# Scores of a spiking recommender on one core: the last time step by pieces, loads by three parts with 24 successive rows per partition

## The chip, the cores and the metric

The kernel runs on one core of a Trainium2 chip. The metric is the device time of one execution in microseconds (us). Before the change it is 1647.41 us, the median of three runs from 1646.87 to 1650.15.

## What is computed

A batch of B = 1024 users has T = 50 item numbers each; a table has N = 100001 items with D = 128 values. The reference, cut to what matters:

```python
emb = emb_table.at[0].set(0.0)
prefix = jnp.cumsum(emb[seq], axis=1)
denom = jnp.minimum(arange(1, T + 1)[None, :], lengths[:, None])
uF = prefix / denom[:, :, None]
y = (uF - uF.mean(axis=0)) * rsqrt(uF.var(axis=0) + 1e-5) * gamma + beta   # over the batch
def step(v, x):                     # 50 steps, one after the other
    v = v + (x - v) / 2.0
    spike = (v >= 1.0)
    return v - spike, spike
scores = spikes.mean(axis=0) @ emb.T          # [1024, 128] @ [128, 100001]
```

The output is 1024 x 100001 float32 values, 409.6 MB.

## The kernel before, in words

**First stage, 50 steps.** D lies on the 128 partitions and the 1024 users on the free axis. For each step `gather` issues eight indirect DMAs from POOL (L198), one for each 128 users. PE transposes each gathered block of 128 x 128 into the running sums `pre[0]` and `pre[1]` (L307), two PSUM tiles of 512 columns. For each half DVE scales the sums to `uF` (L316) and takes batch statistics (L317); it joins them to mean and variance `mv` (L327). ACT takes the square root (L331) and subtracts the mean from all 1024 columns (L332). DVE takes the reciprocal, improves it by one Newton step and makes the scale `a` (L340 to L346, on 128 x 1 columns), ACT applies the scale (`x`, L350), and DVE adds the old potential (`step`, L353), which it holds as `negv = s - v` (L359; L302 in the last step). `s` are the spikes of the step before (L337; L301 in the last step), which `counted` adds up in PSUM by a matmul (L275).

In the last step `s` and `negv` are made whole at the head (L301, L302). At its end the work after `a` goes by three groups of 128, 512 and 384 columns. `countA`, `countB` and `countC` are the final spike counts (`spiked`, L286) that the second stage needs as weights. `warm` (L376) is 16 transposes whose output nobody reads, in the PSUM tile v0.

**Second stage, 98 parts.** The table is cut into parts of 1024 rows (`HALF`); the last has 673. A part in SBUF is turned by PE (L128) and split by ACT and DVE into a high and a low half (`prepare`, L150 and L151), and each of the eight groups of 128 users is multiplied by both (`product`, L158). A product of 128 users by 1024 rows lies in one of four PSUM tiles, and DVE and ACT in turn scale it and write it to `o` in SBUF (L467 and L469). When all parts of a chunk are written for a group of users, one store on SP's queue brings `o` to memory (L167). `WIDTHS` gives the parts of each chunk: 4 chunks of 2, 4 of 3, 11 of 6 and 3 of 4. From the ninth chunk on, three buffers `o` of six parts take turns.

**Loads.** `fetch` loads table rows (L106). The first 38 parts (`HELD`) are loaded on SP's queue in the first stage, the other 60 by loads of three parts on ACT's queue, in the user groups n = 1 and n = 4 of the chunks. Partition p gets rows 8p to 8p + 7 of each part, which is 4096 bytes in a row in memory. So a transposed part has its columns in the order of k and p, and the split reads PSUM in an order that puts them right (`views`). The end of the last part is loaded by single rows of 512 bytes (L115, L120).

**Order.** The program fixes the order on each engine by hand. DMAs from SP and ACT use eight DMA semaphores in turn: an issue waits until the DMA that had its semaphore before it has landed.

The functions that the change touches:

Of the kernel before, what the change touches and what calls it, by code (L numbers as in the profile page):

```python
# [12 lines left out]
F32 = mybir.dt.float32  # L13
# [5 lines left out]
ALU = mybir.AluOpType  # L19

P = 128
BN_EPS = 1e-5
V_TH = 1.0
HALF = 1024
KQ = HALF // P
BANK = 512
GROUP = 6
AHEAD = 6
LATE = 2
HELD = AHEAD * GROUP + LATE  # L30

WIDTHS = 4 * [2] + 4 * [3] + 11 * [6] + [4, 4, 4]
NARROW, MIDDLE = 4, 8


# [1 line left out]
def rec_kernel(  # L37
# [9 lines left out]
    nc = tc.nc  # L47
    B, T = seq.shape
    N, D = table.shape
    NB = B // P  # L50
# [13 lines left out]
    countA = const.tile([P, P], F32R, tag="countA", name="countA")  # L64
# [9 lines left out]
    parts = -(-N // HALF)  # L74
    assert sum(WIDTHS) == parts
    rows = {}
    split = {}

    free = [
        [embp.tile([P, HALF], F32R, tag=f"{x}{i}", name=f"{x}_{i}") for x in ("hi", "lo")] for i in range(2)  # L80
    ]

    def size(q):
        return min(HALF, N - q * HALF)
# [14 lines left out]
    def fetch(r, q, n):  # L99

        engine = nc.sync if q < HELD else nc.scalar
        k = slot(q)[1]
        n = min(n, parts - q)
        whole = n - (size(q + n - 1) < HALF)
        if whole:
            engine.dma_start(  # L106
                out=r[:, k : k + whole, :],
                in_=table[q * HALF : (q + whole) * HALF, :].rearrange("(q p k) d -> p q (k d)", p=P, k=KQ),
            )
        if whole < n:  # L110
            full, rest = divmod(size(parts - 1), P)
            c1 = (parts - 1) * HALF
            r = r[:, k + whole, :].rearrange("p (k d) -> p k d", d=D)
            if full:
                engine.dma_start(  # L115
                    out=r[:, :full, :],
                    in_=table[c1 : c1 + full * P, :].rearrange("(k p) d -> p k d", p=P),
                )
            if rest:
                engine.dma_start(out=r[:rest, full, :], in_=table[c1 + full * P : N, :])  # L120
# [49 lines left out]
    with ExitStack() as ph:  # L170
# [23 lines left out]

        def gather(t):
            es[t] = gp.tile([P, B], F32, tag="e", name=f"e_{t}")
            for n in range(NB):
                nc.gpsimd.indirect_dma_start(  # L198
                    out=es[t][:, n * P : (n + 1) * P],
                    out_offset=None,  # L200
                    in_=table,
                    in_offset=bass.IndirectOffsetOnAxis(ap=idx[:, n, t : t + 1].bitcast(U32), axis=0),
                )
# [81 lines left out]
        def spiked(out, cs, v):  # L285
            nc.vector.scalar_tensor_tensor(out, v, V_TH, count[:, cs], ALU.is_ge, ALU.add)  # L286

        whole = slice(0, B)
        halves = [slice(h * BANK, (h + 1) * BANK) for h in range(B // BANK)]
        v = None  # L290
# [3 lines left out]
        for t in range(T):  # L294
            last = t == T - 1
            if t + 1 < T:
                gather(t + 1)
            e = es.pop(t)
            if last:
                s = lp.tile([P, B], BF16, tag="s", name=f"s_{t - 1}")  # L300
                nc.vector.tensor_single_scalar(s, v, V_TH, ALU.is_ge)  # L301
                nc.vector.tensor_tensor(negv, s, v, ALU.subtract)  # L302
            uF = up.tile([P, B], F32, tag="uF", name=f"uF_{t}")
            bs = sp.tile([P, B // BANK, 6], F32, tag="bs", name=f"bs_{t}")
            for h, cs in enumerate(halves):
                for k in range(0, BANK, P):
                    nc.tensor.matmul(  # L307
                        pre[h][:, k : k + P],
                        lhsT=e[:, h * BANK + k : h * BANK + k + P],
                        rhs=ident,  # L310
                        start=False,
                        stop=last,
                        is_transpose=True,
                        skip_group_check=True,
                    )
                nc.vector.scalar_tensor_tensor(uF[:, cs], rlen[:, cs], 1.0 / (t + 1), pre[h], ALU.max, ALU.mult)  # L316
                nc.vector.bn_stats(bs[:, h, :], uF[:, cs])  # L317
            if not last:
                correct(t + 1, l)
            else:  # L320

                counted(t - 1, s)
                count = once.tile([P, B], F32, tag="zT", name="count")
                for h, cs in enumerate(halves):
                    nc.scalar.copy(count[:, cs], sums[h])
            mv = sp.tile([P, 2], F32, tag="mv", name=f"mv_{t}")
            nc.vector.bn_aggr(mv, bs.rearrange("p h s -> p (h s)"))  # L327


            r = sp.tile([P, 1], F32, tag="r", name=f"r_{t}")  # L330
            nc.scalar.activation(r, mv[:, 1:2], AF.Sqrt, bias=eps)  # L331
            nc.scalar.activation(uF, uF, AF.Identity, bias=mv[:, 0:1], scale=-1.0)  # L332


            if t and not last:
                s = lp.tile([P, B], BF16, tag="s", name=f"s_{t - 1}")
                nc.vector.tensor_single_scalar(s, v, V_TH, ALU.is_ge)  # L337
                counted(t - 1, s)

            nc.vector.reciprocal(r, r)  # L340
            q = sp.tile([P, 1], F32, tag="q", name=f"q_{t}")
            nc.vector.tensor_mul(q, r, r)
            nc.vector.scalar_tensor_tensor(q, mv[:, 1:2], BN_EPS, q, ALU.add, ALU.mult)
            nc.vector.tensor_scalar(q, q, -0.5, 1.5, ALU.mult, ALU.add)
            a = sp.tile([P, 1], F32, tag="a", name=f"a_{t}")
            nc.vector.tensor_scalar(a, q, r, hgb[:, 0:1], ALU.mult, ALU.mult)  # L346


            def x(vt, cs):
                nc.scalar.activation(vt, uF[:, cs], AF.Identity, bias=hgb[:, 1:2], scale=a)  # L350

            def step(vt, cs):
                nc.vector.scalar_tensor_tensor(vt, negv[:, cs], -0.5, vt, ALU.mult, ALU.add)  # L353

            if not last:
                vt = vp.tile([P, B], F32, tag=f"v{t % 2}", name=f"v_{t}")
                x(vt, whole)
                if t:
                    nc.vector.tensor_tensor(negv, s, v, ALU.subtract)  # L359
                step(vt, whole)  # L360
                v = vt
                if t + 2 < T:
                    l = only(t + 2)

                if t in (T - 8, T - 6):
                    q = (t - T + 8) // 2
                    prepare(q, vp.tile([P, HALF], F32, tag="v1", name=f"pt_{q}"))
                    fetch(tiles[0], GROUP + q, 1)
                    rows[GROUP + q] = tiles[0][:, q, :]
# [1 line left out]

        warm = vp.tile([P, HALF], F32, tag="v0", name="warm")
        for k in range(2 * KQ):
            nc.tensor.transpose(warm[:, k % KQ * P : (k % KQ + 1) * P], ident, ident)  # L376
        vC = vp.tile([P, B - BANK - P], F32, tag="v1", name="vC")
        groups = [
            (slice(0, P), pre[0][:, :P], countA),
            (slice(P, P + BANK), pre[1], countB),  # L380
            (slice(P + BANK, B), vC, countC),
        ]
        for cs, vt, _ in groups:
            x(vt, cs)
        cs, vt, first = groups[0]
        step(vt, cs)
        spiked(first, cs, vt)
        for cs, vt, _ in groups[1:]:
            step(vt, cs)
        for cs, vt, c in groups[1:]:  # L390
# [26 lines left out]
    to_fetch = HELD  # L417
# [5 lines left out]
    for c, W in enumerate(WIDTHS):  # L423
# [30 lines left out]
        for n in range(NB):  # L454
# [5 lines left out]
            for q in range(q0, q1):  # L460
                h0 = (q - q0) * HALF
                hw = size(q)
                po = psum.tile([P, HALF], F32, tag="ps", name=f"po_{n}_{q}")
                for k0 in range(0, hw, BANK):
                    product(po[:, k0 : k0 + BANK], q, n, k0, min(BANK, hw - k0))
                if turn % 2 == 0:
                    nc.vector.tensor_scalar_mul(o[:, h0 : h0 + hw], po[:, :hw], 1.0 / T)  # L467
                else:
                    nc.scalar.mul(o[:, h0 : h0 + hw], po[:, :hw], 1.0 / T)  # L469
                turn += 1  # L470
                if c == 0 and n == 1:
                    store(n, q * HALF, o[:, h0 : h0 + hw])
                if n == NB - 1:
                    free.append(split.pop(q))
                    ready()
# [5 lines left out]
            if n in (1, 4) and c >= MIDDLE and to_fetch < parts:  # L481
                g, k = slot(to_fetch)
                if k or to_split >= (g - 1) * GROUP + LATE:
                    if k == 0:
                        r = group(g)
                    fetch(r, to_fetch, GROUP // 2)
                    to_fetch += GROUP // 2
        assert to_split == q2
        q0 = q1

# [18 lines left out]
```

## Time and profile before

The profiled execution took 1574.98 us, of which the span from the first to the last instruction is 1573.2 us. It is 72.4 us below the median of the three runs; the profile doesn't show why.

| what | where | time |
|---|---|---|
| first stage, up to the first store's issue | timeline | 511.6 us |
| POOL busy with gathers (L198) | page, part 5 | 377.8 us, 400 of 945 ns |
| DVE evictions (L467) | page, part 5 | 464.1 us, 391 of 1220 ns |
| ACT evictions (L469) | page, part 5 | 388.1 us, 391 of 1019 ns |
| stores, DMA queue q1 | page, part 3 | 429.81 MB with the first loads |
| late loads, DMA queue q10 | page, part 3 | 31.28 MB |
| memory rate from 718 to 1436 us | windows | 424 GB/s, DMA share 1.00 |

A row of part 5 gives line, engine, operation, output and input with shapes, and count; then busy time and the mean of one; then the idle time before them and who ended it. In part 2 each digit is a slice of 39.3 us.

### The profile page before, as it was taken

Reading aid. Unit: us, or ns where it says so; the run is one execution under the profiler, and the core shown is the slowest. Engines: PE = TensorE matmul, PEld = TensorE weight load, DVE = VectorE, ACT = ScalarE, POOL = GpSimd, SP = SyncE. Lnnn points to the kernel's source line nnn. Section 1 sums busy time; section 2 is a strip of 40 time slices with the busy share of each in tenths; the row PEclk is TensorE's granted clock in tenths of the full one; section 3 lists DMA queues with packets and bytes.
Section 4 is the critical chain, followed back from the end, with each engine's and each line's share of the span. In section 5 each row is a group of like instructions: output and inputs, shape, how many; then the busy total and the mean of one; then the engine's idle time right before and its main releaser. Section 6 shows DMA issues by size and latency. Waiting matters only on the chain.

```text
span 1573.2 us, 12601 instructions
## 1 busy us (share of the span) xinstructions
PE 1147.9 (73%) x4538; PEld 817.6 (52%) x4548; DVE 942.1 (60%) x1161; ACT 630.6 (40%) x700; POOL 378.5 (24%) x406
## 2 busy tenths in 40 slices
PE   4555555555555998889878878887888778777885
PEld 2222222222233776668667666666666667665763
DVE  4777777777777665667555545545555555554553
ACT  2322222222233554555444444444444444443442
POOL 6777777777776000000000000000000000000000
PEclk9999999999999999999999999999999999999998
DMA  9622222222221999999999999999999999999898
GB/s 338 247 53 53 53 53 52 53 53 53 53 79 45 385 416 403 423 417 402 426 429 428 430 427 424 421 415 428 418 428 423 414 428 410 426 424 426 362 423 371
DMA packets 54859, 488.14 MB, mean 310 GB/s; under 512 B 12139, under 2 KB 12940, under 8 KB 32524
## 3 DMA queue, kind: packets, MB, share of 16 engines
q1 hardware_dynamic: 33424, 429.81, 65.1%
q0 software_dynamic: 12800, 26.24, 6.3%
q10 hardware_dynamic: 8572, 31.28, 5.0%
q8 instruction: 36, 0.59, 0.1%
q14 instruction: 27, 0.22, 0.0%
HBM read 77.69 MB, written 409.60 MB: 310 GB/s over the span
## 4 chain that ended last, share of the span: by engine, by line
DMA 50%; POOL 19%; PE 11%; issue 10%; ACT 5%; DVE 4%; another core or an unknown queue 0%; DVEq 0%; ACTq 0%; SPq 0%; POOLq 0%
DMA scores<-o 46%; POOL e L198 19%; PE po L158 10%; ACT o L469 4%; DMA e<-in_L_rec_emb_table,idx 3%; DVE o L467 2%; DMA rows<-in_L_rec_emb_table 2%; PE pt L128 1%; PE pre L307 0%; ACT pairs L150 0%; DVE s L337 0%; DVE bs L317 0%; DVE uF L316 0%; DVE pairs L151 0%; DMA idx<-in_r_seq 0%
## 5 line engine op out<-in xcount | busy, mean ns | idle before, releaser
L467 DVE TENSOR_SCALAR o<-po 128x1024 f32<-128x1024 f32 x391 | 464.1, 1220 | 354.3 <-DMA scores<-o 314.5
L469 ACT ACTIVATE o<-po 128x1024 f32<-128x1024 f32 (+1 forms) x391 | 388.1, 1019 | 548.9 <-DMA scores<-o 336.2
L198 POOL DMA_INDIRECT e<-in_L_rec_emb_table,idx x400 | 377.8, 945 | 124.5 <-issue 116.4
L158 PE MATMUL po<-pairs,countB 128*128 128x512 f32 x1136 | 304.6, 415 | 69.0 <-ACT o L469 52.1
L158 PEld LDWEIGHTS po<-pairs,countB 128*128 128x128 f32 x1136 | 218.5, 197 | 132.0 <-ACT o L469 66.8
L307 PE MATMUL pre<-ident,e 128*128 128x128 f32 x400 | 156.2, 452 | 152.4 <-DMA e<-in_L_rec_emb_table,idx 149.0
L158 PE MATMUL po<-pairs,countC 128*128 128x512 f32 x852 | 230.4, 416 | 49.3 <-ACT o L469 49.3
L158 PEld LDWEIGHTS po<-pairs,countC 128*128 128x128 f32 x852 | 163.6, 198 | 94.2 <-ACT o L469 60.5
L307 PEld LDWEIGHTS pre<-ident,e 128*128 128x128 f32 x400 | 79.2, 200 | 246.1 <-DMA e<-in_L_rec_emb_table,idx 223.6
L151 DVE TENSOR_TENSOR pairs<-pt,pairs 128x1024 fp32r<-128x1024 f32 x71 | 86.3, 1222 | 91.3 <-ACT pairs L150 91.2
L331 ACT ACTIVATE r<-mv,eps 128x1 f32<-128x1 f32 x50 | 14.7, 295 | 305.5 <-DVE mv L327 305.5
L316 DVE SCALAR_TENSOR_TENSOR uF<-rlen,pre 128x512 f32<-128x512 f32 x100 | 68.4, 684 | 108.3 <-PE pre L307 108.2
L128 PE MATMUL pt<-ident,rows 128*128 128x128 f32 x782 | 111.7, 290 | 9.7 <-ACT o L469 5.1
L128 PEld LDWEIGHTS pt<-ident,rows 128*128 128x128 f32 x782 | 100.3, 152 | 29.9 <-issue 8.8
L158 PE MATMUL po<-hi,countB 128*128 128x512 f32 x216 | 89.5, 414 | 15.8 <-ACT o L469 12.6
L264 PE MATMUL pre<-zT,l 128*128 128x512 f32 x100 | 78.1, 783 | 18.9 <-DVE uF L316 18.8
L275 PE MATMUL sums<-s,ident_h 128*128 128x512 bf16 x88 | 45.4, 607 | 60.6 <-DVE s L337 60.6
L158 PE MATMUL po<-lo,countB 128*128 128x512 f32 x216 | 86.5, 402 | 0.0
L158 PE MATMUL po<-pairs,countA 128*128 128x512 f32 x284 | 71.7, 395 | 9.3 <-ACT o L469 9.2
L150 ACT CAST pairs<-pt 128x1024 fp32r<-128x1024 f32 x71 | 71.8, 1012 | 15.0 <-PE pt L128 14.8
L158 PE MATMUL po<-hi,countC 128*128 128x512 f32 (+1 forms) x162 | 67.8, 418 | 11.7 <-ACT o L469 11.7
L350 ACT ACTIVATE v<-uF,hgb,a 128x1024 f32<-128x1024 f32 x49 | 59.2, 1208 | 37.6 <-DVE a L346 37.5
(76 smaller groups left out, 841.9 us busy)
## 6 DMA issues: line engine op xcount, KB each, us to landing
scores<-o SPq DMA_DIRECT2D x88, 3072.0 KB, 20.3
scores<-o SPq DMA_DIRECT2D x32, 1536.0 KB, 8.9
scores<-o SPq DMA_DIRECT2D x16, 2048.0 KB, 12.6
scores<-o SPq DMA_DIRECT2D x30, 1024.0 KB, 8.6
rows<-in_L_rec_emb_table ACTq DMA_DIRECT2D x19, 1536.0 KB, 29.3
rows<-in_L_rec_emb_table SPq DMA_DIRECT2D x6, 3072.0 KB, 25.3
scores<-o SPq DMA_DIRECT2D x8, 1872.5 KB, 11.3
e<-in_L_rec_emb_table,idx POOLq DMA_INDIRECT x400, 2.5
```

Source lines behind the costliest of these rows:

```text
L128: nc.tensor.transpose(pt[:, k0 : k0 + kw], r[:kw, k0 : k0 + D], ident[:kw, :kw])
L150: nc.scalar.copy(vh, vp)
L151: nc.vector.tensor_tensor(vl, vp, vh.bitcast(F32), ALU.subtract)
L158: nc.tensor.matmul(po[:, :kw], lhsT=counts[n], rhs=part[:, k0 : k0 + kw], start=j == 0, stop=j == 1,)
L198: nc.gpsimd.indirect_dma_start(out=es[t][:, n * P : (n + 1) * P], out_offset=None, in_=table, in_offset=bass.IndirectOffsetOnAxis(ap=idx[: ...
L264: nc.tensor.matmul(pre[h], lhsT=l, rhs=zT[:, h * BANK : (h + 1) * BANK], start=t == 0, stop=False, skip_group_check=True,)
L275: nc.tensor.matmul(sums[h], lhsT=ident_h, rhs=s[:, h * BANK : (h + 1) * BANK], start=t == 0, stop=t == T - 2, skip_group_check=True,)
L307: nc.tensor.matmul(pre[h][:, k : k + P], lhsT=e[:, h * BANK + k : h * BANK + k + P], rhs=ident, start=False, stop=last, is_transpose=True, ...
L316: nc.vector.scalar_tensor_tensor(uF[:, cs], rlen[:, cs], 1.0 / (t + 1), pre[h], ALU.max, ALU.mult)
L350: nc.scalar.activation(vt, uF[:, cs], AF.Identity, bias=hgb[:, 1:2], scale=a)
L467: nc.vector.tensor_scalar_mul(o[:, h0 : h0 + hw], po[:, :hw], 1.0 / T)
L469: nc.scalar.mul(o[:, h0 : h0 + hw], po[:, :hw], 1.0 / T)
```

## The change

The diff, without its comments and blank lines:

```diff
+TRIO = GROUP // 2
-WIDTHS = 4 * [2] + 4 * [3] + 11 * [6] + [4, 4, 4]
+WIDTHS = 4 * [2] + 4 * [3] + 12 * [6] + [3, 3]
...
+    trios = range(HELD, parts - TRIO)
+    assert (parts - HELD) % TRIO == 0
...  (in fetch)
+        if q in trios:
+            engine.dma_start(
+                out=r[:, k : k + n, :],
+                in_=table[q * HALF : (q + n) * HALF, :].rearrange("(p r) d -> p (r d)", p=P),
+            )
+            return
...  (in gather)
-            for n in range(NB):
+            order = list(range(NB))
+            if t == T - 1:
+                order.append(order.pop(NB // 2))
+            for n in order:
...
+        thirds = [slice(0, P), slice(P, P + BANK), slice(P + BANK, B)]
+        def negated(cs):
+            nc.vector.tensor_tensor(negv[:, cs], s[:, cs], v[:, cs], ALU.subtract)
...  (in the step, if last)
-                nc.vector.tensor_tensor(negv, s, v, ALU.subtract)
             uF = up.tile([P, B], F32, tag="uF", name=f"uF_{t}")
-            bs = sp.tile([P, B // BANK, 6], F32, tag="bs", name=f"bs_{t}")
-            for h, cs in enumerate(halves):
-                for k in range(0, BANK, P):
+            pieces = halves if not last else halves[:1] + [slice(B - 3 * P, B), slice(BANK, BANK + P)]
+            bs = sp.tile([P, len(pieces), 6], F32, tag="bs", name=f"bs_{t}")
+            for j, cs in enumerate(pieces):
+                h = cs.start // BANK
+                if last and j == len(pieces) - 1:
+                    counted(t - 1, s)
+                for c0 in range(cs.start, cs.stop, P):
+                    k = c0 - h * BANK
...  (transpose of the block, then L316 and L317 on the columns of the piece)
             else:
-                counted(t - 1, s)
                 count = once.tile([P, B], F32, tag="zT", name="count")
...
             nc.scalar.activation(r, mv[:, 1:2], AF.Sqrt, bias=eps)
+            ve = sp.tile([P, 1], F32, tag="ve", name=f"ve_{t}")
+            nc.vector.tensor_scalar_add(ve, mv[:, 1:2], BN_EPS)
...
+            if last:
+                negated(thirds[0])
             nc.vector.reciprocal(r, r)
             q = sp.tile([P, 1], F32, tag="q", name=f"q_{t}")
-            nc.vector.tensor_mul(q, r, r)
-            nc.vector.scalar_tensor_tensor(q, mv[:, 1:2], BN_EPS, q, ALU.add, ALU.mult)
+            nc.vector.scalar_tensor_tensor(q, r, ve, r, ALU.mult, ALU.mult)
...  (after the last step)
-        warm = vp.tile([P, HALF], F32, tag="v0", name="warm")
+        warm = vp.tile([P, HALF], F32, tag="v1", name="warm")
...
+        groups = list(zip(thirds, (pre[0][:, :P], pre[1], vC), (countA, countB, countC)))
+        negated(thirds[1])
         for cs, vt, _ in groups:
             x(vt, cs)
         cs, vt, first = groups[0]
         step(vt, cs)
         spiked(first, cs, vt)
+        negated(thirds[2])
...  (second stage, eviction)
+                to, of = o[:, h0 : h0 + hw], po[:, :hw]
+                if q in trios:
+                    j = (q - HELD) % TRIO
+                    trio = o[:, h0 - j * HALF : h0 + (TRIO - j) * HALF]
+                    to = trio.rearrange("b (p r) -> b p r", p=P)[:, :, j * KQ : (j + 1) * KQ]
+                    of = po.rearrange("b (p k) -> b p k", k=KQ)
                 if turn % 2 == 0:
-                    nc.vector.tensor_scalar_mul(o[:, h0 : h0 + hw], po[:, :hw], 1.0 / T)
+                    nc.vector.tensor_scalar_mul(to, of, 1.0 / T)
                 else:
-                    nc.scalar.mul(o[:, h0 : h0 + hw], po[:, :hw], 1.0 / T)
+                    nc.scalar.mul(to, of, 1.0 / T)
```

It has three parts.

*Loads by three parts.* For the parts 38 to 94 a load of three parts gives partition p the rows 24p to 24p + 23 of the 3072 rows: 12288 bytes in a row in memory instead of three times 4096. Each of the three parts in SBUF then holds 8 of every 24 rows. The products of such a part belong in runs of 8 columns, 24 apart, and the evictions write them there in `o`. The stores read `o` in a row as before. The last load (parts 95 to 97) stays as it was.

*Widths.* Twelve chunks of six parts and two of three, so that a group of three parts always lies in one chunk.

*The last step.* The block of users 512 to 639 is gathered last, and the statistics are taken over 512, 384 and then 128 columns. The count of the step before goes ahead of the last block's transpose. The subtraction for `negv` is made in three pieces: the first before the reciprocal, the second after `a`, the third after `countA`. `warm` moves to the tile v1. In all 50 steps the variance plus epsilon is made beside ACT's square root (`ve`), and the Newton step has one multiply less after the reciprocal.

More of the change, by code (lines that the diff above doesn't have):

```diff
@@ L301, in rec_kernel @@
                 nc.vector.tensor_single_scalar(s, v, V_TH, ALU.is_ge)
-                nc.vector.tensor_tensor(negv, s, v, ALU.subtract)
             uF = up.tile([P, B], F32, tag="uF", name=f"uF_{t}")
-            bs = sp.tile([P, B // BANK, 6], F32, tag="bs", name=f"bs_{t}")
-            for h, cs in enumerate(halves):
-                for k in range(0, BANK, P):
+            pieces = halves if not last else halves[:1] + [slice(B - 3 * P, B), slice(BANK, BANK + P)]
[6 more added lines that the diff above has]
+                    k = c0 - h * BANK
                     nc.tensor.matmul(
                         pre[h][:, k : k + P],
-                        lhsT=e[:, h * BANK + k : h * BANK + k + P],
+                        lhsT=e[:, c0 : c0 + P],
                         rhs=ident,
@@ L315, in rec_kernel @@
                     )
-                nc.vector.scalar_tensor_tensor(uF[:, cs], rlen[:, cs], 1.0 / (t + 1), pre[h], ALU.max, ALU.mult)
-                nc.vector.bn_stats(bs[:, h, :], uF[:, cs])
+                nc.vector.scalar_tensor_tensor(
+                    uF[:, cs],
+                    rlen[:, cs],
+                    1.0 / (t + 1),
+                    pre[h][:, cs.start - h * BANK : cs.stop - h * BANK],
+                    ALU.max,
+                    ALU.mult,
+                )
+                nc.vector.bn_stats(bs[:, j, :], uF[:, cs])
             if not last:
@@ L358, in rec_kernel @@
                 if t:
-                    nc.vector.tensor_tensor(negv, s, v, ALU.subtract)
+                    negated(whole)
                 step(vt, whole)
@@ L377, in rec_kernel @@
         vC = vp.tile([P, B - BANK - P], F32, tag="v1", name="vC")
[L378 to L382, printed above, removed]
+        groups = list(zip(thirds, (pre[0][:, :P], pre[1], vC), (countA, countB, countC)))
+        negated(thirds[1])
         for cs, vt, _ in groups:
@@ L485, in rec_kernel @@
                         r = group(g)
-                    fetch(r, to_fetch, GROUP // 2)
-                    to_fetch += GROUP // 2
+                    fetch(r, to_fetch, TRIO)
+                    to_fetch += TRIO
         assert to_split == q2
```

## The prediction

> **What bounds the kernel now.** I read the page's slices and queues first, then its groups and issues, then the windows, the DMA queue's own waits, and last the timeline of the hand-over between the two stages.
>
> ```profile
> DMA  9622222222221999999999999999999999999898
> GB/s 338 247 53 53 53 53 52 53 53 53 53 79 45 385 416 403 423 417 402 426 429 428 430 427 424 421 415 428 418 428 423 414 428 410 426 424 426 362 423 371
> q1 hardware_dynamic: 33424, 429.81, 65.1%
> q10 hardware_dynamic: 8572, 31.28, 5.0%
> ```
>
> There are two stages. Up to slice 13 (511 us) the DMA engines idle; after it they are at nine tenths or more, except in slice 38. The stores are on q1, the late row loads on q10.
>
> ```profile
> L467 DVE TENSOR_SCALAR o<-po 128x1024 f32<-128x1024 f32 x391 | 464.1, 1220 | 354.3 <-DMA scores<-o 314.5
> L469 ACT ACTIVATE o<-po 128x1024 f32<-128x1024 f32 (+1 forms) x391 | 388.1, 1019 | 548.9 <-DMA scores<-o 336.2
> L198 POOL DMA_INDIRECT e<-in_L_rec_emb_table,idx x400 | 377.8, 945 | 124.5 <-issue 116.4
> rows<-in_L_rec_emb_table ACTq DMA_DIRECT2D x19, 1536.0 KB, 29.3
> scores<-o SPq DMA_DIRECT2D x88, 3072.0 KB, 20.3
> ```
>
> Stage one is POOL: 400 gathers at 0.945 + 0.30 us of issue = 1.25 us, so 10.0 us a step and 500 us in all; its DVE and ACT work hides under that. In stage two both evicting engines wait for stores to free an `o`. The stores are the bound.
>
> ```profile
> core 0: us, PE busy (x) PEld busy (x) DVE busy (x) ACT busy (x) POOL busy (x), PEclk, DMA share, GB/s
> 511.00:525.00 14.00, 13.51 (x63) 10.87 (x62) 10.09 (x11) 7.72 (x9) 0.00 (x0) 1.00 0.79 315
> 718.00:1436.00 718.00, 594.53 (x2601) 469.02 (x2600) 384.48 (x325) 320.98 (x326) 0.00 (x0) 0.94 1.00 424
> 1455.00:1465.00 10.00, 10.00 (x46) 8.39 (x47) 6.60 (x7) 5.57 (x6) 0.00 (x0) 0.83 0.42 177
> ```
>
> From 718 to 1436 the DMA share is 1.00 at 424 GB/s. The one hole is 1455 to 1465: (1 - 0.42) x 10 = 5.8 us of 16 engines. Its cause stands in the queue's waits:
>
> ```profile
> SPq L167 <- DMA rows<-in_L_rec_emb_table: 26.7, 3, 13.1
> rows<-in_L_rec_emb_table ACTq DMA_DIRECT2D x1, 320.0 KB, 50.7
> ```
>
> The last load's 512-byte pieces (L115) are issued at 1411.36 and land at 1462.07. The store that takes the same DMA semaphore next is held on SP until then and issued at 1462.16; its first packet starts at 1463.00.
>
> That hole costs less than it seems. A store is done when its last engine is done, and one engine lags: by 2.0 us behind the median at 719, by 7.9 at 1456 (the store issued at 1448.64: median landing 1456.16, last 1464.03). During the hole that engine still has stores to move; its lag falls to about 1.3 us, and it is that engine which ends the kernel. So the time follows the slow engine's work, and the hole is rest for the other fifteen.
>
> **What the Trainium skill says.** "DMA: Bandwidth & Descriptors", section "Queues, rings and completion order": each engine takes turns between queue rows packet by packet. The trace agrees: a load with 24 packets of 4 KB per engine takes 29.3 us to land, near 24 x (0.924 + 0.162) = 26.1. Same page, "Why a DMA increments its semaphore by 16 and not by 1": the engines finish independently and only the full count means landed; the lag above is that. "Vector Engine (DVE) Microarchitecture Reference", section "5.2 Measured stream behaviour on trn2": a port keeps its full rate if elements come in runs of at least two adjacent 4-byte words starting at 8 bytes, with free hops between; single words 24 apart cost 2.50 ns a column against 1.054. No row of before shows an eviction that writes runs; the new runs are 8 words.
>
> **Part by part.**
> *Loads.* 19 of the 20 late loads go from 3 x 4096 to 1 x 12288 bytes per partition. On each engine (8 partitions): before 19 x 24 = 456 packets, after 152. From the trace's packet records a 4096-byte read takes 162.5 ns; no 12288-byte read is in the trace, the nearest is the 12288-byte store packet, 468.6. Saving 3 x 162.5 - 468.6 = 18.8 ns, x 152 = 2.9 us on each engine, the slow one too. Bounds: 0 (stretches with loads and without run at 425.6 and 425.9 GB/s, so fixed cost per packet may hide) and 5 us if turns between queues cost something; a loss of 3 us if long reads run 4% slower. I take 2.7. A load then lands in about 8 x (0.92 + 0.47) = 11 us. Issue on ACT: 0.375 us today, no dearer with fewer packets.
>
> *Evictions.* 57 parts x 8 = 456 of the 782 write runs of 8. Price nothing by the page, for DVE; for ACT no page bears on it. Cover: a six-part block takes the DMA 8 x 0.924 + 0.975 (two loads per eight blocks, 48 x 0.1625 / 8) = 8.37 us, DVE 3 x 1.22 + 0.75 x 1.22 = 4.6, ACT 3.9, PE about 6.3 (6 x 4 matmuls at 0.23 plus 0.75 transposed parts at 1.03). The cover is gone when an eviction takes (8.37 - 0.92) / 3 = 2.5 us.
>
> *Widths.* 11 x 6 + 3 x 4 becomes 12 x 6 + 2 x 3. Per engine before, 16 stores x 8 x 0.619 + 8 x 8 x 0.570 = 115.7 us; after, 8 x 8 x 0.924 + 8 x 8 x 0.469 + 8 x 8 x 0.415 (10884 bytes, estimated from the 12288 row) = 115.7. Zero. A three-part block needs 2.8 us of PE, 3.8 while it also transposes, against 3.75 of DMA with two blocks queued: hidden. If that cover went, up to 1 us per block in three blocks. After 1436 come 24 KB store packets where 16 KB ones were; the short pieces take turns with them. On the slow engine some 13 turns fall there: 13 x (0.951 - 0.646) = 4 us, landing 1466 instead of 1462, on the old clock. Its stores last longer too: 1453.7 + 2 x 7.4 + 0.4 = 1468.9. Still no idling there, zero.
>
> *Step tail.* `ve` replaces a multiply of 0.16 us in each of 50 steps: in the first 49 hidden by the gathers. In the last step the 1.22 us subtraction at L302 leaves the head, and the chain moves so:
>
> ```profile
> 505.85 0.67 DVE L316 SCALAR_TENSOR_TENSOR uF<-rlen,pre 128x512 f32<-128x512 f32 x1
> 506.55 0.69 DVE L317 BATCH_NORM_STATS2 bs<-uF 128x6 f32<-128x512 f32 x1
> 507.72 1.13 ACT L332 ACTIVATE uF<-uF,mv 128x1024 f32<-128x1024 f32 x1
> 508.63 0.27 DVE L346 TENSOR_SCALAR a<-q,r,hgb 128x1 f32<-128x1 f32 x1
> 511.62 17.51 SPq L167 DMA_DIRECT2D scores<-o  x12
> ```
>
> The last gathered piece is 128 columns: 0.30 + 0.29 us (a 128-column row of L353 is 0.297) instead of 0.67 + 0.69, less 0.12 because DVE is still at the 384-column piece. `mv` is 0.62 earlier. The multiply saved is eaten by L332 and the first `negated` (0.29). The second `negated` (0.69) goes before the first step, so `countA` comes 0.5 earlier, first store 511.1; but `countB` comes 512.25 instead of 511.95, since all three subtractions (0.29 + 0.69 + 0.55) now lie after the last gather. DVE's first eviction at L401 moves from 512.99 to 512.86, and PE, which waits for it until 513.73, goes on 0.13 us earlier. Until 521 the stores wait for products, so PE's restart counts: 0.1 us gained, between +0.3 and -0.5. `warm` moves to the other PSUM tile and ends about 509.5, before it is waited for.
>
> **Sum.** 2.7 + 0.1 = 2.8 us off the profiled 1574.98 (span 1573.2): 1572.2. The median of the runs is 1647.41, 72.4 us above it, and nothing on the page says where; I carry the difference over unchanged: 1644.6, or -0.17%. That lies just inside 0.2% (3.3 us), about what a measurement of this kernel can tell from no change.
>
> **Rivals.**
> *Faster: the hole counts* (0.30). If the other fifteen engines matter, because the slow engine's lag has room elsewhere, and the six-part chunk fills the hole with longer stores: 5.8 + 2.8 = 8.6 us, 1638.8; half of it, 1641.7. For: slice 38 is the only lasting dip. Against: the lag closes by just the time lost, and the short load that holds SP is unchanged.
> *Slower: evictions* (0.09). If ACT or DVE pay for runs at the page's 2.50 ns: 1024 x 2.50 + 153 (1220 less 1067) = 2.71 us; DVE needs 3 x 2.71 + 0.92 = 9.05 us against 8.33, 0.72 x 76 blocks = 55 us: near 1700. It decides from 2.5 us an eviction; runs of 8 speak against.
> *Slower: SP held too long* (0.13). If the short pieces land later than 1468.9, each microsecond idles the slow engine: at 1475, 6 + 0.8 of start latency, less 2.8: 1651.4. It needs 9 us more than I work out to do net harm beyond 0.2%.
> *Loads save nothing* (part of the 0.48 for the forecast): 1647.3, still no change.
>
> **Numbers.** Forecast with its own range 1642.5 to 1647.5: 0.48, of which 0.05 falls below the bound on the fast side. Faster 0.30 + 0.05 = 0.35; slower 0.22; same 0.43. The range 1638.5 to 1651.5 holds forecast, hole and most of the held SP; the eviction case is left out.
>
> **What would show it.** Right: 152 load packets of 12288 bytes per engine near 470 ns, landing near 11 us; L467 and L469 still near 1220 and 1020 ns; share 1.00 from 718 on; first store near 511.1; a hole near 1460 of similar size. Wrong: evictions above 2.4 us; the hole gone and the end earlier by it; or load packets well off 470 ns.

## The result and the profile after

The changed kernel takes 1648.89 us, the median of four runs from 1647.55 to 1649.83; the kernel before took 1648.26 beside it (1646.87 to 1650.15). The ratio is 1.0002, with a 95% interval of 0.9985 to 1.002: no change that can be measured. The forecast was 1644.6, with the largest of its three chances, 0.43, on no change. The time lies inside the wide range of the prediction (1638.5 to 1651.5) and above the narrow one that it gave its own sum (1642.5 to 1647.5).

The profiled execution of the changed kernel took 1648.65 us, with a span of 1646.9. That is 73.7 us more than the span of the profile before, while the medians differ by 0.6. The two profiles can't be subtracted as a whole: this one shows the 72 us that the prediction carried over. First the slices, queue and groups on the page of the changed kernel (L506 and L508 are the evictions L467 and L469 of before, L211 is L198):

```profile
DMA  9511111111112189999999999999999999999899
GB/s 341 214 46 48 47 45 48 48 45 48 48 46 61 46 329 416 404 423 415 405 420 426 428 431 425 422 424 416 415 431 417 427 416 411 431 413 420 358 422 377
q10 hardware_dynamic: 3708, 31.28, 4.8%
L506 DVE TENSOR_SCALAR o<-po 128x1024 f32<-128x1024 f32 x391 | 464.0, 1217 | 361.2 <-DMA scores<-o 304.7
L508 ACT ACTIVATE o<-po 128x1024 f32<-128x1024 f32 x391 | 392.1, 1021 | 548.5 <-DMA scores<-o 322.5
L211 POOL DMA_INDIRECT e<-in_L_rec_emb_table,idx x400 | 377.6, 944 | 184.8 <-issue 113.1
```

Packets on q10 fall from 8572 to 3708. Evictions that write runs of 8 cost what they cost before, to 3 ns. The hole in slice 38 has moved by the 73 us and stays.

Now the windows of the changed kernel: the first stage, and a stretch deep in the second.

```profile
core 0: us, PE busy (x) PEld busy (x) DVE busy (x) ACT busy (x) POOL busy (x), PEclk, DMA share, GB/s
0.00:582.00 582.00, 227.99 (x651) 135.44 (x652) 367.30 (x673) 151.10 (x211) 378.26 (x406) 0.53 0.27 80
790.00:1508.00 718.00, 600.50 (x2599) 477.96 (x2598) 384.11 (x326) 322.15 (x325) 0.00 (x0) 0.91 1.00 423
```

The first store is issued at 582.33 us, against 511.62 in the profile before: 70.7 of the 73.7 us lie in the first stage. From the first store to the end the changed kernel takes 1064.5 us, against 1061.6 before. So the second stage, which the loads were to shorten, is 3 us longer. The waits of the changed kernel say who is late in the first stage (who waited, for what: us in total, times, longest):

```profile
PE pre L277 <- DVE uF L342: 205.6, 65, 10.1
DVE uF L342 <- remote: 160.6, 32, 12.9
POOL e L211 <- remote: 61.5, 17, 5.4
```

DVE's scaling of the sums waits 160.6 us for something that the profile can't name, 12.9 us at the longest, and POOL 61.5 us. Before, POOL waited 124.5 - 116.4 = 8.1 us in all for anything but its own issuing.

### The profile page after: what moved, and what is told of

Its sections match the earlier page's. It is cut to its first block, busy times and chain, and to the rows that moved or that the text cites. A ratio compares the mean times of both kernels' runs of the same rounds, so it can differ in the third digit from the quotient of the medians.

```text
span 1646.9 us, 12619 instructions
## 1 busy us (share of the span) xinstructions
PE 1121.2 (68%) x4548; PEld 838.8 (51%) x4548; DVE 944.5 (57%) x1165; ACT 633.7 (38%) x700; POOL 378.3 (23%) x406
## 4 chain that ended last, share of the span: by engine, by line
DMA 40%; PE 17%; DVE 16%; another core or an unknown queue 9%; POOL 6%; ACT 6%; issue 5%; ACTq 0%; DVEq 0%; SPq 0%; POOLq 0%
DMA scores<-o 39%; PE po L168 16%; POOL e L211 6%; ACT o L508 5%; DVE bs L350 3%; DVE uF L342 3%; DVE v L387 2%; DVE s L370 2%; DVE negv L305 2%; DVE o L506 1%; PE pt L138 1%; DMA e<-in_L_rec_emb_table,idx 1%; DVE a L380 0%; DVE mv L358 0%
## 5 line engine op out<-in xcount | busy, mean ns | idle before, releaser
L506 DVE TENSOR_SCALAR o<-po 128x1024 f32<-128x1024 f32 x391 | 464.0, 1217 | 361.2 <-DMA scores<-o 304.7
L508 ACT ACTIVATE o<-po 128x1024 f32<-128x1024 f32 x391 | 392.1, 1021 | 548.5 <-DMA scores<-o 322.5
L211 POOL DMA_INDIRECT e<-in_L_rec_emb_table,idx x400 | 377.6, 944 | 184.8 <-issue 113.1
L168 PE MATMUL po<-pairs,countB 128*128 128x512 f32 x1136 | 313.0, 423 | 74.1 <-ACT o L508 58.7
L168 PEld LDWEIGHTS po<-pairs,countB 128*128 128x128 f32 x1136 | 225.7, 204 | 137.1 <-ACT o L508 71.1
L168 PE MATMUL po<-pairs,countC 128*128 128x512 f32 x852 | 236.4, 424 | 44.6 <-ACT o L508 44.6
L168 PEld LDWEIGHTS po<-pairs,countC 128*128 128x128 f32 x852 | 167.8, 203 | 90.1 <-ACT o L508 55.2
L277 PEld LDWEIGHTS pre<-zT,l 128*128 128x128 f32 x100 | 28.0, 281 | 287.2 <-issue 169.8
L342 DVE SCALAR_TENSOR_TENSOR uF<-rlen,pre 128x512 f32<-128x512 f32 (+1 forms) x101 | 68.1, 674 | 169.7 <-remote 160.6
L333 PE MATMUL pre<-ident,e 128*128 128x128 f32 x400 | 102.5, 422 | 19.5 <-DMA e<-in_L_rec_emb_table,idx 16.5
L333 PEld LDWEIGHTS pre<-ident,e 128*128 128x128 f32 x400 | 85.4, 223 | 52.1 <-DMA e<-in_L_rec_emb_table,idx 26.3
L168 PE MATMUL po<-hi,countB 128*128 128x512 f32 x216 | 89.8, 416 | 16.9 <-ACT o L508 15.5
L288 PE MATMUL sums<-s,ident_h 128*128 128x512 bf16 x98 | 49.6, 609 | 75.1 <-DVE s L370 46.7
```

Of the source, the lines that this page charges most:

```text
L168: nc.tensor.matmul(po[:, :kw], lhsT=counts[n], rhs=part[:, k0 : k0 + kw], start=j == 0, stop=j == 1,)
L211: nc.gpsimd.indirect_dma_start(out=es[t][:, n * P : (n + 1) * P], out_offset=None, in_=table, in_offset=bass.IndirectOffsetOnAxis(ap=idx[: ...
L277: nc.tensor.matmul(pre[h], lhsT=l, rhs=zT[:, h * BANK : (h + 1) * BANK], start=t == 0, stop=False, skip_group_check=True,)
L288: nc.tensor.matmul(sums[h], lhsT=ident_h, rhs=s[:, h * BANK : (h + 1) * BANK], start=t == 0, stop=t == T - 2, skip_group_check=True,)
L333: nc.tensor.matmul(pre[h][:, k : k + P], lhsT=e[:, c0 : c0 + P], rhs=ident, start=False, stop=last, is_transpose=True, skip_group_check=True,)
L506: nc.vector.tensor_scalar_mul(to, of, 1.0 / T)
```

## The experiments

Each ratio is to the kernel before, run in turn with it on the same chip, with its 95% interval. The chips were not equal: the kernel before takes 1647.44 us on the chip of the first four experiments, 1574.82 on that of the next four, 1650.69 on that of the last four. So ratios are compared, and of spans only the parts after the first store.

**The kernel before, unchanged.** No edit.

> The kernel before once more, for a trace that can be laid beside that of the changed kernel. Theory (clock): the runs near 1648 us have TensorE at half clock in the first stage, as the trace of the changed kernel shows (0.53), and the first stage then takes about 72 us longer: first store near 582 us, time from first store to end near 1062 us. Rival (transfers): the 72 us lie in slower transfers of the second stage: first store near 512 us, 1132 us from there to the end.

Measured: 0.9999 [0.9988, 1.001]. Its profile on this chip has the first store at 582.6 us and 1062.3 us after it. The long first stage is therefore no work of the change. Its windows, with the columns of those of the changed kernel above:

```profile
0.00:582.00 582.00, 230.16 (x649) 134.86 (x650) 362.32 (x669) 150.79 (x211) 378.34 (x406) 0.68 0.27 80
790.00:1508.00 718.00, 593.23 (x2600) 467.73 (x2599) 384.36 (x325) 320.86 (x326) 0.00 (x0) 0.94 1.00 423
```

**The loads, the widths and the evictions alone**, with the old last step:

```diff
-WIDTHS = 4 * [2] + 4 * [3] + 11 * [6] + [4, 4, 4]
+WIDTHS = 4 * [2] + 4 * [3] + 12 * [6] + [3, 3]
+        if q in trios:        # in fetch: 24 rows per partition
+            engine.dma_start(out=r[:, k : k + n, :], in_=...)
+                if q in trios:     # evictions in runs of 8, 24 apart
```

> The loads by three parts, the widths and the evictions in runs alone, on the old step. The prediction's step (a 12288-byte load packet takes 469 ns) gives 2.7 us less, ratio 0.9984. Theory now: the packets take 497 ns, as in the trace of the changed kernel, 3 x 162.5 = 487 before, so nothing is saved: between 0 and +1.5 us, ratio 1.000 to 1.001.

Measured: 1.0025 [1.0013, 1.0037], or +4.1 us. The half of the change that was to give 2.7 us costs 4. The loads' row in the issues of its page (count, size, median us to landing; before it was 29.3):

```profile
rows<-in_L_rec_emb_table ACTq DMA_DIRECT2D x19, 1536.0 KB, 16.9
```

**The last step alone**, with the old loads and widths:

```diff
-    trios = range(HELD, parts - TRIO)
+    trios = ()
-WIDTHS = 4 * [2] + 4 * [3] + 12 * [6] + [3, 3]
+WIDTHS = 4 * [2] + 4 * [3] + 11 * [6] + [4, 4, 4]
```

> The last step by pieces and the shorter Newton step alone, with the old loads and widths. The prediction's step gives 0.1 us less (between -0.5 and +0.3), ratio 1.000. If the half clock makes the steps follow their own chain instead of the gathers, one multiply less after the reciprocal could count in each of 50 steps, though it stands before it instead: up to 0.2 us x 50 = 10 us less, ratio 0.994.

Measured: 0.9987 [0.998, 0.9995], or -2.1 us. The two halves nearly cancel: 0.0025 - 0.0013 = 0.0012.

**PE kept busy in the first stage**, to see whether the clock makes it long on this chip. The added matmuls have zero weights and add nothing to the counts:

```diff
+                    if not last and h * BANK + k < B - P:
+                        busy(t, h)      # two bf16 matmuls of 512 columns, weights zero
```

> The kernel before with two matmuls of zero weights (bf16, 512 columns, added into the spike counts) behind each of the first seven transposes of a step, 14 a step in 49 steps, to keep TensorE busy in the first stage. Theory (clock): the clock stays near 1.0 in the first stage, steps take 10.0 us as in the first trace, first store near 512 us, time near 1576 us, ratio 0.956. Rival (transfers, or a stall that has nothing to do with the clock): no change or slower by the added work, ratio 1.00 or above.

Measured: 1.0039 [1.0025, 1.0054], or +6.4 us; the first store is at 590.9 instead of 582.6. The clock rose to 0.80 and nothing was won. Of the 8.3 us, 7.5 lie ahead of the first `mv` (28.1 us instead of 20.7; no run shows why); the steps after it take 11.39 us on average, as in the kernel before (11.38). The kernel before, of the first experiment, says the same without any added work. Two windows of its first stage:

```profile
20.00:160.00 140.00, 55.15 (x142) 29.56 (x142) 82.61 (x153) 34.39 (x48) 93.73 (x100) 1.00 0.43 148
200.00:560.00 360.00, 143.49 (x410) 85.00 (x408) 232.60 (x423) 95.28 (x132) 243.38 (x259) 0.53 0.20 50
```

Its clock is 1.00 up to 183 us and about half after that. From `mv` to `mv`, its first 14 steps take 11.3 us each and the other 35 take 11.4. The next experiment shows the same from the other side.

**The widths alone:**

```diff
-WIDTHS = 4 * [2] + 4 * [3] + 11 * [6] + [4, 4, 4]
+WIDTHS = 4 * [2] + 4 * [3] + 12 * [6] + [3, 3]
```

> The widths alone: twelve chunks of six parts and two of three, loads and evictions as before. The prediction's step gives 0, ratio 1.000. Theory now: of the 4.1 us that loads, widths and evictions cost together, the load packets take 2.1 us (152 x 504 ns against 456 x 163 ns on each engine), and the rest, 2.0 us, is the end of the second stage, so the ratio is 1.001. Rival: all 4.1 us are the loads', ratio 1.000.

Measured: 0.9999 [0.9991, 1.0007]. The widths cost nothing, as forecast. This execution also happened to have half the clock through its first stage; a window of its profile, and the same window of the kernel before on a chip that takes 1575 us:

```profile
20.00:500.00 480.00, 250.93 (x587) 116.04 (x596) 346.63 (x635) 141.37 (x197) 362.94 (x385) 0.50 0.27 84
```

```profile
20.00:500.00 480.00, 250.73 (x587) 116.29 (x596) 346.80 (x635) 141.31 (x197) 362.90 (x385) 1.00 0.29 85
```

Clock 0.50 against 1.00, the same work done in the window, spans of 1573.3 and 1573.2. Half the clock in the first stage costs nothing here, and full clock saves nothing on the chip with the long stage. So the clock isn't what makes that stage 72 us longer.

**The loads without the runs.** The kernel of the second experiment, whose evictions write 1024 columns in a row again; so in parts 38 to 94 the output's columns are in another order:

```diff
-                if q in trios:
-                    to = trio.rearrange("b (p r) -> b p r", p=P)[:, :, j * KQ : (j + 1) * KQ]
-                    of = po.rearrange("b (p k) -> b p k", k=KQ)
```

> Loads by three parts and widths as in the changed kernel, old step, but the evictions write in a row as before; the columns of parts 38 to 94 then stand in another order in the output. Theory (runs cost nothing, rows at 1217 and 1021 ns): as with the runs, ratio 1.0025. Rival (the runs in o slow the evictions or the stores that read them): ratio 1.000.

Measured: 1.0020 [1.0012, 1.0028], or +3.1 us. The loss is still there without the runs and, by the experiment before, not in the widths. What is left is the loads. The packet records say how (reads of the late loads on queue q10, all 16 engines; these numbers are counted from the records, not shown on the page):

| | 4096-byte reads, before | 12288-byte reads, this kernel |
|---|---|---|
| median | 159 ns | 460 ns |
| mean | 162.5 | 502.0 |
| mean of those that start up to 5.5 us after a load's issue | 174 | 595 |
| from 5.5 to 7.5 us | 160 | 501 |
| later than 7.5 us | 161 | 462 |
| later than 7.5 us, with 11 or more reads under way | 170 | 465 |
| sum per engine, all reads of 4096 bytes or more | 76.7 us | 79.1 us |

At the median a large packet takes 460 ns and would save 3 x 159 - 460 = 17 ns, times 152, or 2.6 us on each engine. But the mean is 502, and the sum is 2.4 us larger than before. The long reads are slow at the beginning of each load, in the first 4 us after its first packet. The number of engines that read at once doesn't explain it: reads that start late take 465 ns with 11 or more reads under way, and early ones (2.5 to 7.5 us after the issue) take 520 ns with 7 or fewer. Why a load begins slowly isn't shown.

In the second stage this kernel takes 3.2 us more than the kernel before (1064.8 against 1061.6). The reads alone don't account for it. In the experiment with more DMA updates below, whose late loads and stores are those of before, they take 79.7 us per engine, the stores take less, and the time stays. Reads and stores together, from the first store on, take 1047.0 to 1048.3 us per engine in the ten profiles with 4096-byte late loads and 1048.8 to 1049.9 in the four with 12288-byte ones, 1.7 us more on average. The rest isn't traced. The loss builds up while the loads run: counted from the first store, the loads of n = 1 are issued 0.4 us later than before at 400 us, 1.6 at 804 and 2.6 at 872, and the last load (parts 95 to 97, unchanged) 3.2 us later (902.5 against 899.3), as much as the end.

**The hole closed.** In the kernel before, the end of the last part is loaded in pieces of 2560 bytes instead of 512:

```diff
-                    in_=table[c1 : c1 + full * P, :].rearrange("(k p) d -> p k d", p=P),
+                    in_=table[c1 : c1 + full * P, :].rearrange("(p k) d -> p k d", p=P),
...  (in views and prepare: this part is split in two pieces, in the order that the load gives)
```

> The kernel before with the end of the last part loaded as five rows in a row for each partition (2560 bytes) instead of single rows of 512, and split in two pieces in the order that this gives. The short pieces no longer hold a DMA semaphore for 50 us, so the hole near 1460 (1530 in later runs) should close: DMA share near 1.00 there. Theory (the slow engine ends the kernel and works through the hole): ratio 0.9990 to 1.0005, and the lag of the slowest engine at the end larger than before, 7 us instead of 4. Rival (the hole counts): 5.8 us less, ratio 0.9965.

Measured: 1.0000 [0.9992, 1.0008]. A window of its profile, at the place of the hole (DMA share 0.42, 177 GB/s before):

```profile
1455.00:1465.00 10.00, 9.70 (x44) 8.16 (x45) 6.59 (x7) 5.24 (x7) 0.00 (x0) 0.83 0.93 391
```

Share 0.93 at 391 GB/s: the 5.8 us of 16 engines are used, and the kernel is not faster. In exchange the slowest engine is further behind. Just after the hole a store lands at 1469.7 us before, with its slowest engine 1.3 us behind the median; with the hole closed it lands at 1469.9, 6.8 us behind. At the last stores it is 5.3 us against 3.7. The fifteen others worked earlier and waited for it longer.

**More DMA updates in the first stage.** Three loads of 4 KB on SP's queue in each of 38 steps, whose data nobody uses:

```diff
+            for u in range(3 if 2 <= t < T - 10 else 0):
+                nc.sync.dma_start(out=tiny[...], in_=lengths.rearrange("(p n) -> p n", p=P))
```

> The kernel before with three more loads of 4 KB on SP's idle queue in each of 38 steps of the first stage (the users' lengths, which nobody reads), spread over 16 engines: 48 more semaphore increments a step beside some 160. Theory (the first stage is held by the rate at which semaphore increments are served, 11.37 us / 160 = 71 ns each): 48 x 0.071 x 38 = 130 us more, ratio 1.08. Rival (it is held by something else on PE, and SP's queue is free): ratio 1.00.

Measured: 1.0002 [0.9993, 1.001]. No effect, but on the chip whose first stage is short. It shows that these updates don't make a short stage long; it says nothing of the chips whose stage is long already.

**The changed kernel again**, with more runs, on a chip with the long first stage.

> The changed kernel once more, beside the others of this call. If the parts add up, loads at +3.1 us (between +1.9 and +6.1 in two calls), widths at 0 and the last step at -2.1 us: +1 us, ratio 1.0006 (0.9995 to 1.002). On a chip where the first stage ends near 511 us, the prediction's -2.8 us would be 0.9982.

Measured: 1.0013 [1.0006, 1.0021], or +2.1 us. So the change is a small loss, as the two halves add up (0.0012), and inside the interval of the first result. On the chip with the short first stage the whole change wasn't timed; its loads alone cost 3.1 us there.

**The last step alone again**, the kernel of the third experiment, and **the last step by pieces with the old Newton step**:

```diff
-            nc.vector.scalar_tensor_tensor(q, r, ve, r, ALU.mult, ALU.mult)
+            nc.vector.tensor_mul(q, r, r)
+            nc.vector.scalar_tensor_tensor(q, mv[:, 1:2], BN_EPS, q, ALU.add, ALU.mult)
```

> The last step by pieces and the shorter Newton step alone, the same kernel as e3_step. Where the first stage ends near 582 us: 0.9987 again. Where it ends near 511 us and TensorE is at full clock at the hand-over, the prediction's 0.1 us (to 0.5): 0.9997 to 1.0000. If the clock at the first products makes the difference (TensorE at half clock there in the old step, at full clock in the new), 0.999 also on a chip that is not slow in the first stage but has the half clock.

> The last step by pieces alone, with the old Newton step in all 50 steps. Theory (the gain of e3_step lies in the last step): the same ratio as e12_step in this call. Rival (the shorter chain after the reciprocal counts in each step): ratio 1.000, no gain left.

Measured: 0.9984 [0.9977, 0.9991] and 0.9985 [0.9974, 0.9995]: -2.6 and -2.5 us. The saved multiply is worth nothing that shows; the gain is the order of the last step. Both of these kernels beat the kernel before and, beside it on one chip, the changed kernel (1.0013). They weren't timed on the chip with the short first stage.

Where its gain lies is seen in PE's timeline at the hand-over between the stages (start, duration, line and operation, idle before and who ended it). The kernel before, of the first experiment:

```profile
577.70 1.48 PE L376 MATMUL warm<-ident 128*128 128x128 f32 x6
581.25 0.47 PE L158 MATMUL sums<-hi,countA 128*128 128x512 f32 x1 [2.08 <-ACT pre L350]
...
582.72 0.62 PE L158 MATMUL po<-hi,countA 128*128 128x512 f32 x1
583.14 0.63 PE L158 MATMUL po<-lo,countA 128*128 128x512 f32 x1
583.56 0.63 PE L158 MATMUL po<-hi,countB 128*128 128x512 f32 x1
```

The kernel with the last step alone:

```profile
579.97 3.61 PE L410 MATMUL warm<-ident 128*128 128x128 f32 x16
583.76 0.47 PE L168 MATMUL sums<-hi,countA 128*128 128x512 f32 x1 [0.18 <-ACT pre L384]
...
585.23 0.39 PE L168 MATMUL po<-hi,countA 128*128 128x512 f32 x1
585.46 0.39 PE L168 MATMUL po<-lo,countA 128*128 128x512 f32 x1
585.89 0.47 PE L168 MATMUL po<-hi,countB 128*128 128x512 f32 x1
```

Before, `warm` ends early and PE idles 2.08 us. The products start at 0.39 us, but 1.5 us later they take 0.62, for 3.45 us at about half the clock. With the new order `warm` runs to within 0.18 us of the products and they keep 0.39. The other profiles from the chips with the long stage agree. With the old order PE idles 2.1 to 2.7 us there and 7 or 8 of the first products take over 0.55 us (four profiles); with the new order it idles 0.2 to 0.6 us and at most 2 do (five profiles).

Two sums from the records fit: from `mv` of the step before to `mv` of the last 9.17 us instead of 10.01 (-0.84), and from the first store's issue to that of an early six-part store 206.8 or 206.9 in all five instead of 207.7 to 208.0 in all four (-1.0). Together -1.8 of the -2.1 to -2.6. On the chip with the short stage the old order has 206.8 already.

**The new addresses with small packets.** The kernel of the second experiment, each load of three parts split into three DMAs of 4096-byte packets, 12288 bytes apart in memory:

```diff
-            engine.dma_start(out=r[:, k : k + n, :], in_=table[...].rearrange("(p r) d -> p (r d)", p=P))
+            src = table[q * HALF : (q + n) * HALF, :].rearrange("(p r) d -> p (r d)", p=P)
+            for j in range(n):
+                engine.dma_start(out=r[:, k + j, :], in_=src[:, j * HALF : (j + 1) * HALF])
```

> Loads by three parts, widths and evictions in runs, old step, but each load of three parts as three DMAs of one part each: the same 24 successive rows for each partition, read in packets of 4096 bytes that lie 12288 bytes apart. Theory (a 12288-byte packet takes one turn of three against the stores, so more engines read at once, and reads then take 574 to 607 ns instead of 460): with small packets the loads spread out again and cost what they did before, ratio 1.0000 (0.9993 to 1.0006). Rival (the addresses, or the evictions and stores behind them, cost the time): 1.002 as in e6_plain.

Measured: 1.0004 [0.9992, 1.0017]. The same evictions, widths and addresses cost nothing that can be told once the packets are 4096 bytes. These take 161.4 ns again and 76.2 us per engine, and the last load starts at 899.2 us after the first store, without delay. Beside it on the same chip the 12288-byte packets cost 1.0013 / 0.9984, or 0.0029 (the changed kernel over the last step alone). So it is the size of the packet that costs most of it. A small cost of the rest isn't excluded: the interval reaches 1.0017, and the second stage of this profile takes 1063.4 us, against 1062.3 for the kernel before of the first experiment and 1065.7 for the second experiment. The reason expected for this result, that small packets keep fewer engines reading at once, isn't what the table above shows.

## Why the prediction was right, and where it wasn't

The verdict, no change, was right, and the reason given for it was not: two terms were off in opposite directions and nearly cancel. That they do is luck.

*The loads: wrong in sign.* Forecast -2.7, measured +3.1 (without the runs) and +4.1 us. The step that failed is the price of the packet: "no 12288-byte read is in the trace, the nearest is the 12288-byte store packet, 468.6". At the median a read does take 460 ns, but in the kernels with these loads they average 497 to 504, because each load begins slowly. 502 / 468.6 is 7% slower than assumed, and 502 against 3 x 162.5 = 487.5 for the small ones is a loss of 14.5 ns instead of a gain of 18.8. The bound "a loss of 3 us if long reads run 4% slower" named the case with a wrong sum: 1.04 x 468.6 = 487.3 ns only uses up the gain, and a loss of 3 us takes 8%.

The prediction quoted the Trainium skill, "DMA: Bandwidth & Descriptors", section "Queues, rings and completion order", for engines that take turns packet by packet. It used that for the landing time, and the trace agrees: fewer turns bring the landing from 29.3 us down to 15.9 to 16.9. The forecast of 11 us fits the reads alone (11.4 us from the first packet to the end of the last, in the kernel without the runs); it left out the 3.5 us from the issue to the first packet. The small packets (1.0004) show the size to be the cause of the loss; what makes the long reads slow at the beginning of a load stays open.

*Evictions: right.* 1217 and 1021 ns, against 1220 and 1019; with the new widths and no runs they are 1217 and 1022. For DVE the trace agrees with "Vector Engine (DVE) Microarchitecture Reference", section "5.2 Measured stream behaviour on trn2"; the slow-eviction rival fell at once.

*Widths: right.* Forecast zero, 0.9999 measured.

*Step tail: right in sign, far too small.* Forecast -0.1 with bounds of +0.3 and -0.5, measured -2.1 to -2.6. `mv` came 0.84 earlier instead of 0.62 (the prediction's own terms give 0.65). The step that failed is "until 521 the stores wait for products, so PE's restart counts: 0.1 us gained", with `warm` costed at nothing: both were read from a profile with a short first stage, where `warm` ends 0.21 us ahead of the products and the clock is 1.00 anyway:

```profile
510.26 0.47 PE L158 MATMUL sums<-hi,countA 128*128 128x512 f32 x1 [0.21 <-ACT pre L350]
```

With the long first stage the old order leaves PE idle for 2.08 us there. That the idling takes the clock down is argued from its place just ahead, in four profiles of four; that the clock is down, and what the products lose by it, is in the rows above. On the chip with the short first stage no run shows this gain.

*The hole: right.* "The time follows the slow engine's work, and the hole is rest for the other fifteen": closing it gave 1.0000. The rival with a chance of 0.30 is refuted, and the slowest engine is 5.5 us further behind just after the hole, nearly the 5.8 us that the others gain, as the reason given requires.

*SP held too long: longer than forecast, and without loss.* In the changed kernel the longest wait of SP's queue for row loads is 17.3 us, against 13.1 before (in all 18.1 against 26.7):

```profile
SPq L177 <- DMA rows<-in_L_rec_emb_table: 18.1, 2, 17.3
```

In the profile of the loads without the runs, which is from the chip with the short first stage, the short pieces land at 1470.8 us, later than the 1466 that was worked out. Yet the slowest engine isn't seen to idle: SP is free at 1470.85, and that engine ends its earlier store at 1471.7. The 3.2 us are also all there when the last load is issued, some 40 us before this wait begins.

*The 72.4 us carried over: right, without knowing what they were.* They are a longer first stage, in the kernel before as in the changed one, on two of the three chips of these experiments.

## What to carry to other kernels

A read packet is priced from reads, and from the mean over a whole load, its beginning included. The price of a store packet of that size (468.6 ns), or the median of the reads themselves (460 ns), missed the sign here; the mean was 502. Larger packets save little where the fixed cost is small: at the median 17 ns for three packets made one, which the slow first 4 us of each load more than used up. A hole on the fast engines is free while one slow engine ends the kernel, but an idle stretch of PE just ahead of work that others wait for may not be: soon after 2 us of idling the products ran 3.45 us at about half the clock.

## What the runs showed of the hardware

Chips differ in the first stage by 72 us with one program: steps of 9.92 us on average on one, and of 11.30 to 11.46 on others, mostly one of 18 to 19 us and then two of 7.5 or 7.6. The trace of the kernel before on such a chip shows one stall, all engines:

```profile
295.87 0.47 PE L307 MATMUL pre<-ident,e 128*128 128x128 f32 x1 [0.77 <-DMA e<-in_L_rec_emb_table,idx]
...
299.58 0.69 DVE L316 SCALAR_TENSOR_TENSOR uF<-rlen,pre 128x512 f32<-128x512 f32 x1 [3.97 <-issue]
...
300.41 0.76 PE L264 MATMUL pre<-zT,l 128*128 128x512 f32 x1 [4.06 <-DVE uF L316]
...
303.31 0.94 POOL L198 DMA_INDIRECT e<-in_L_rec_emb_table,idx  x1 [0.30 <-issue]
307.27 0.69 DVE L316 SCALAR_TENSOR_TENSOR uF<-rlen,pre 128x512 f32<-128x512 f32 x1 [6.28 <-remote]
307.51 0.94 POOL L198 DMA_INDIRECT e<-in_L_rec_emb_table,idx  x1 [3.25 <-remote]
```

The last transpose in the trace ends at 296.34, yet DVE scales the second half at 307.27, after 6.28 us of waiting, and POOL stops for 3.25 us. On these chips 1231 of the 6400 increments of the gathers' semaphores are recorded (1240 in the changed kernel), on the other chip 6400, and during this stall, with no PE instruction in the trace from 301.2 to 308.0 us, PE's recorded semaphore updates stand at multiples of 0.70 us from each other (302.35, 305.15, 306.55, 307.25). Late semaphore updates would fit all of it, but no run here tests that on such a chip. The clock is excluded (half of it cost nothing on the other chip, and 14 steps at full clock were as long on this one), and so is the change (the kernel before has the same stage); the cause stays open.
